# Moving the halves of a record from ScalarE's scaled block one-hots to VectorE's scaled place one-hots in a graph kernel

## The chip, the cores and the metric

The kernel runs on one core of a Trainium2 chip. The metric is the device time of one launch in microseconds. The engines are called PE (TensorE), DVE (VectorE), ACT (ScalarE), POOL (GpSimd) and SP (SyncE), as the profile calls them; PEld is PE's loading of the stationary operand.

## What is computed

20,000 nodes carry 256 numbers each, and 340,000 edges are sorted by their destination. A relational layer is applied twice, then an attention layer:

```python
def _rgcn_layer(x, W, self_w, b, src, dst, edge_type, num_nodes):
    xW = jnp.einsum('ni,rio->rno', x, W)
    msg = xW[edge_type, src]
    agg = jax.ops.segment_sum(msg, dst, num_segments=num_nodes)
    return agg + x @ self_w + b
...
x = layernorm(x + rgcn(relu(rgcn(x))))          # 8 edge types
# attention: here the segments are the sources (row = src), the gathered rows those of dst
e = leaky_relu(hl[row] + hr[col]); att = softmax of e within each row; out[row] += att * h[col]
x = layernorm(x + out)
```

The relational layers sum over edges that end in a node, the attention layer over edges that start in one. So the edges, given in order of destination, must also be brought into order of source.

## The kernel before

**Rounds one and two** are the two relational layers (`by_chunks`). The edges lie in 2657 columns ("tiles") of 128, and 16 tiles make a chunk. For each tile POOL gathers 128 rows by an indirect DMA (L536), 20 tiles ahead in 24 buffers. PE multiplies the gathered rows by one-hots of destination and type that DVE makes (L556), summing into PSUM (L653). ACT and DVE copy the finished sums (L578, L576). PE then multiplies them by the weights: L588 turns the chunk's own rows, L591 (ACT) copies them, L596 and L600 are the products. In round one `use` goes on with L723 to L731, in round two with L762 to L796.

**The order by source** (`ordered`) runs beside the rounds, a piece at a time: after most tiles `pace` lets the generator `side` advance by one `yield`, four times in five tiles in round one from some tile on, five times in eight in round two. The stage that the change touches is `write`, called `the write stage` below. It works on lots of three tiles, and each lot takes three such steps. The sources fall into 157 blocks of 128 nodes; a record is a pair of node and source place in one integer, cut into two halves `hi` and `lo` that fp16 holds exactly. For one tile, with edges on the partitions:

- `blocks_of` (L849, DVE) makes `b`, the one-hot of an edge's block: 128x157 fp16 for each of the three tiles, in one instruction of 471 columns. `b` has 4 buffers.
- `rank` (L1005, L1006, PE) counts, by two products into `pr`, how many edges of the same block come before each edge.
- `place_of` (DVE) takes that count out of `pr` at the edge's block (L1026, three times), takes 128 off where it passes 127 (L1029, L1030), and makes `a`, the one-hot of the place, 128x384 fp16 for a whole lot (L1032). `a` has 3 buffers.
- `parts` (ACT) makes `two`: `b` times `hi` (L1016) and `b` times `lo` (L1017), for each tile; 7 buffers.
- `bring` (PE) adds the transposed `a` times `two` into `pl`, 314 columns for each tile (L1044): every half of a record lands at its place and block.
- `finish` joins the halves and turns and stores a group's records when all its tiles are in.

`pi`, the row of column numbers that `a` and `b` compare with, lies in PSUM as f32. All instructions of an engine run in the order in which the program gives them; the order is written out by hand (`manual_schedule`). In `write` the order for lot m is: `parts(m + 1, 0)` and where a group begins `begin`; a step of `finish`; end of step; `blocks_of(m + 2)`, `parts(m + 1, 1)`, a step of `finish`; end of step; `bring(m)`, `parts(m + 1, 2)`, `rank(m + 1)`, `place_of(m + 1)`; end of step. So PE brings a lot one lot's time after DVE was asked for its places.

**Attention** follows the rounds: for each of 157 blocks POOL gathers 17 tiles of rows (L1252), and PE, DVE and ACT work through them (L1262 to L1399). The change doesn't touch it.

Of the kernel before, what the change touches and what calls it, by code (L numbers as in the profile page):

```python
# [38 lines left out]
FP16 = mybir.dt.float16  # L39
AF = mybir.ActivationFunctionType  # L40
ALU = mybir.AluOpType
# [6 lines left out]
P = 128  # L48
# [13 lines left out]
LOT = 3  # L62
# [4 lines left out]
def gnn_kernel(  # L67
# [17 lines left out]
    nc = tc.nc  # L85
# [5 lines left out]
    NB = (N + P - 1) // P  # L91
# [24 lines left out]
    G = -(-COLS // GT)  # L116
# [686 lines left out]
    class ordered:  # L803
# [171 lines left out]
        def write(self, sp, ps, pi):  # L975
            k = self.k
            lots = self.lots
            held = sp.tile([P, NB], F32, name="held", bufs=1)
            nc.vector.memset(held, 0.0)
            group, made, ranked, later = {}, {}, {}, []  # L980
            pl = [None]

            def begin(g):


                x = ps.tile([P, 512], F32, name="pr")[:, :3 * NB].rearrange("p (a b) -> p a b", a=3)
                nc.tensor.matmul(x[:, 0, :], self.below16, self.count_all[:, g, :], start=True, stop=False)
                of = self.ident16[:, g:g + 1].to_broadcast([P, P])
                nc.tensor.matmul(x[:, 0, :], of, self.place16, start=False, stop=True)
                nc.tensor.matmul(x[:, 1, :], of, self.place16, start=True, stop=True)  # L990
                nc.tensor.matmul(x[:, 2, :], of, self.cross16, start=True, stop=True)
                start = sp.tile([P, NB], FP16, name="start")
                nc.scalar.copy(start, x[:, 0, :])
                cross = sp.tile([P, NB], F32, name="cross")
                nc.scalar.copy(cross, x[:, 2, :])
                mine = sp.tile([P, NB], F32, name="mine")
                nc.vector.tensor_scalar(mine, x[:, 1, :], self.row, None, op0=ALU.is_le)
                group[g] = start, cross, mine

            def rank(m):  # L1000
                g, i, n, _ = lots[m]
                pr = ps.tile([P, 512], F32, name="pr")[:, :LOT * NB].rearrange("p (x b) -> p x b", x=LOT)
                self.pending = True
                for x in range(n):
                    nc.tensor.matmul(pr[:, x, :], self.below16, made[m][:, x, :], start=True, stop=False)  # L1005
                    nc.tensor.matmul(pr[:, x, :], self.ident16[:, i + x:i + x + 1].to_broadcast([P, P]), group[g][0],  # L1006
                                     start=False, stop=True)
                ranked[m] = pr

            def parts(m, x):  # L1010
                g, i, n, _ = lots[m]
                if x >= n:
                    return
                c = g + G * (i + x)
                two = sp.tile([P, 2, NB], FP16, name="two", bufs=2 * LOT + 1)
                nc.scalar.activation(two[:, 0, :], made[m][:, x, :], AF.Copy, scale=k["hi"][:, c:c + 1])  # L1016
                nc.scalar.activation(two[:, 1, :], made[m][:, x, :], AF.Copy, scale=k["lo"][:, c:c + 1])  # L1017
                ranked[m, x] = two

            def place_of(m):  # L1020
                g, i, n, _ = lots[m]
                pr = ranked.pop(m)
                r = sp.tile([P, LOT], F32, name="r")
                for x in range(n):
                    dump = sp.tile([P, NB], FP16, name="dump")
                    nc.vector.tensor_tensor_reduce(out=dump, in0=pr[:, x, :], in1=made[m][:, x, :], scale=1.0,  # L1026
                                                   scalar=0.0, op0=ALU.mult, op1=ALU.max, accum_out=r[:, x:x + 1])
                over = sp.tile([P, LOT], F32, name="rover")
                nc.vector.tensor_scalar(over[:, :n], r[:, :n], float(P), -float(P), op0=ALU.is_ge, op1=ALU.mult)  # L1029
                nc.vector.tensor_add(r[:, :n], r[:, :n], over[:, :n])  # L1030
                a = sp.tile([P, LOT, P], FP16, name="a16", bufs=3)
                nc.vector.tensor_tensor(a[:, :n], pi[:, :P].unsqueeze(1).to_broadcast([P, n, P]),  # L1032
                                        r[:, :n].unsqueeze(2).to_broadcast([P, n, P]), op=ALU.is_equal)
                ranked[m] = a

            def bring(m):
                g, i, n, of = lots[m]
                if i == 0:
                    while later:
                        one()  # L1040
                    pl[0] = ps.tile([P, 512], F32, name="pl")[:, :2 * NB].rearrange("p (a b) -> p a b", a=2)
                a = ranked.pop(m)
                for x in range(n):
                    nc.tensor.matmul(pl[0].rearrange("p a b -> p (a b)"), a[:, x, :],  # L1044
                                     ranked.pop((m, x)).rearrange("p a b -> p (a b)"),
                                     start=(i + x == 0), stop=(i + x == of - 1))
                made.pop(m)
                if i + n == of:
                    later.extend(finish(g, pl[0]))
# [47 lines left out]
            def one():  # L1097
                if later:
                    later.pop(0)()

            begin(0)
            for m in (0, 1):
                if m < len(lots):
                    made[m] = self.blocks_of(sp, pi, lots[m])
            rank(0)
            place_of(0)
            for x in range(LOT):
                parts(0, x)
            for m in range(len(lots)):
                more = m + 1 < len(lots)  # L1110
                self.pending = False
                if more:
                    parts(m + 1, 0)

                    if lots[m + 1][1] == 0:
                        begin(lots[m + 1][0])
                        self.pending = True
                one()
                yield
                self.pending = False  # L1120
                if m + 2 < len(lots):
                    made[m + 2] = self.blocks_of(sp, pi, lots[m + 2])
                if more:
                    parts(m + 1, 1)
                one()
                yield
                bring(m)
                if more:
                    for x in range(2, LOT):
                        parts(m + 1, x)  # L1130

                    rank(m + 1)
                    place_of(m + 1)
                yield
# [62 lines left out]
    def attention():  # L1197
        with tc.tile_pool(name="ac", bufs=1) as cp, tc.tile_pool(name="ag", bufs=4) as gp, \
# [204 lines left out]
            def step(i):  # L1403
# [29 lines left out]
                if b and not a:  # L1433

                    weights(b)
                    for t in range(0, b["n"] + 1, 6):
                        weigh_few(b, list(range(t, min(t + 6, b["n"] + 1))))
                        sums(b, range(t, min(t + 6, b["n"] + 1)))
                    if c:
                        sums(c, [17])  # L1440
                        finish(c)
                        measure(c)
                        write(c)
                    finish(b)
                    measure(b)
                    write(b)
                    return
# [19 lines left out]
                for n in range(1, 10):  # L1467
                    if b:
                        sums(b, [n])
                        weigh(b, [n + 4] + ([14, 15] if n == 9 else []))  # L1470
                    if a:
                        greatest(a, (n + 2) // 4, (n + 2) % 4)
                        if n == 5:
                            turned_hots(a)
                    if n in (2, 4, 6, 8):
                        load_ob(i + 2, n // 2)
                    if c and n == 1:
                        measure(c)
                    if c and n == 4:
                        write(c)  # L1480
# [303 lines left out]
    with tc.tile_pool(name="rows", bufs=1) as keep:  # L1784
        k = {}
# [35 lines left out]
```

## Time and profile before

| | |
|---|---|
| time, median of 3 runs | 10404.4 us (10398.89 to 10406.65) |
| profiled execution: its own time | 14109.72 us |
| its span, first to last instruction | 14107.9 us |
| first and last gather of round one and two (L536) | 67.2 and 8681.5 us |
| write stage, first and last product L1044 | 2016 and 8375 us |
| first gather of attention (L1252) | 8724.7 us |
| busy in the span: PE, PEld, DVE, ACT, POOL | 10231.6, 7774.8, 7641.1, 6176.7, 7657.7 us |
| granted TensorE clock, mean | 0.849 of full speed |

The profiled execution took 1.356 times as long as the runs that were timed without the profiler. A duration below is one of the profiled execution. Busy time of PE is modelled, since matmuls overlap; where a rate is wanted, starts are subtracted from starts.

### The profile page before, as it was taken

What the parts mean: (1) busy time and instruction counts of PE and PEld (TensorE: products, weight loads), DVE (VectorE), ACT (ScalarE), POOL (GpSimd) and SP (SyncE); (2) the same over time, 40 slices, a digit from 0 to 9 for tenths busy, and PEclk for the clock granted to TensorE, in tenths of its full rate; (3) what the DMA queues carried; (4) which work ended last, traced back from release to release, by engine and by line L of the source; (5) the groups of instructions that cost most, each with busy time, mean ns of one, the idle gap of its engine ahead of it and who ended that gap; (6) DMA issues with size and microseconds to landing.
All of it is one profiled execution on the core that took longest, in us unless ns stands there. A gap on an engine that the chain in (4) does not pass through costs nothing. (4 is left out here: it accounts for less than half of the span.)

```text
span 14107.9 us, 225925 instructions
## 1 busy us (share of the span) xinstructions
PE 10231.6 (73%) x78029; PEld 7774.8 (55%) x78029; DVE 7641.1 (54%) x21279; ACT 6176.7 (44%) x19534; POOL 7657.7 (54%) x8057
## 2 busy tenths in 40 slices
PE   6888888888887888888888885555555555555555
PEld 5777777777776666766676664333333333333333
DVE  4455555555555555555555542555555555555555
ACT  2211124444443333333333331656656666656656
POOL 5665666665565555555555555444444444444443
PEclk8998999999998999999999997777777777777777
DMA  6654544454444445554555454333333333333332
GB/s 187 181 144 139 143 139 142 142 142 141 141 141 137 142 142 144 143 145 140 143 145 143 143 146 134 92 97 95 101 96 96 100 97 99 97 97 97 98 98 81
DMA packets 859356, 1788.95 MB, mean 127 GB/s; under 512 B 200612, under 2 KB 521746, under 8 KB 858050
## 3 DMA queue, kind: packets, MB, share of 16 engines
q0 software_dynamic: 464336, 1396.47, 36.0%
q1 hardware_dynamic: 387490, 371.40, 8.4%
q8 instruction: 613, 10.04, 0.3%
q10 hardware_dynamic: 6368, 6.54, 0.1%
q14 instruction: 549, 4.50, 0.1%
HBM read 1638.71 MB, written 135.15 MB: 126 GB/s over the span
## 5 line engine op out<-in xcount | busy, mean ns | idle before, releaser
L1252 POOL DMA_INDIRECT g<-table3s,to x2657 | 2565.0, 965 | 2795.4 <-PE po L1362 1547.0
L536 POOL DMA_INDIRECT g<-h2s,idx x2657 | 2517.8, 948 | 1889.1 <-PE a L653 1084.8
L653 PE MATMUL a<-s,g 128*128 128x184 bf16 (+14 forms) x37024 | 3180.2, 231 | 137.7 <-issue 123.6
L1348 ACT ACTIVATE g<-g 128x64 f32<-128x64 f32 x9984 | 2620.4, 336 | 1047.1 <-issue 1024.3
L600 PE MATMUL pm<-wt,to 128*128 128x256 f32 x10624 | 3020.0, 408 | 8.2 <-issue 7.9
L536 POOL DMA_INDIRECT g<-xs,idx x2305 | 2195.3, 952 | 1445.9 <-PE a L653 786.5
L1306 DVE CUSTOM_DVE_ANT_0 dump<-pr,pen 128x768 bf16<-128x768 f32 x1876 | 1654.4, 908 | 2109.4 <-remote 1659.7
L653 PEld LDWEIGHTS <-g 128*128 128x128 bf16 x35352 | 2487.4, 101 | 452.2 <-issue 198.8
L1303 PE MATMUL pr<-hpt,pick 128*128 128x512 bf16 (+2 forms) x3752 | 1007.5, 355 | 2219.3 <-issue 1124.2
L1362 PE MATMUL po<-g,s 128*128 128x260 f32 x5314 | 2014.4, 477 | 99.5 <-DVE g L1354 83.5
L600 PEld LDWEIGHTS pm<-wt,to 128*128 128x128 f32 x10624 | 1902.5, 199 | 231.8 <-issue 53.9
L1303 PEld LDWEIGHTS <-pick 128*128 128x128 bf16 x3752 | 388.1, 103 | 2812.9 <-issue 2697.2
L578 ACT COPY to<-a 128x512 f32<-128x512 f32 x996 | 564.2, 586 | 2979.5 <-PE a L653 2466.3
L1026 DVE CUSTOM_DVE_ANT_0 dump<-pr,b 128x157 f16<-128x157 f32 x2657 | 713.6, 320 | 1958.2 <-PE pr L1006 777.5
L1016 ACT ACTIVATE two<-b,hi 128x157 f16<-128x157 f16 x2657 | 1121.1, 422 | 410.5 <-DVE b L849 214.5
L1362 PEld LDWEIGHTS po<-g,s 128*128 128x128 f32 x5314 | 1003.5, 229 | 522.8 <-issue 179.1
L849 DVE TENSOR_TENSOR b<-pi,kb 128x471 f16<-128x471 f32 (+1 forms) x1798 | 1113.0, 634 | 274.0 <-PE pr L891 103.1
L1017 ACT ACTIVATE two<-b,lo 128x157 f16<-128x157 f16 x2657 | 1099.2, 414 | 0.0
L556 DVE TENSOR_TENSOR s<-pi,code 128x1600 bf16<-128x1600 f32 (+1 forms) x622 | 1022.2, 1644 | 0.0
L596 PE MATMUL pm<-wt,ot 128*128 128x256 f32 x1328 | 506.7, 518 | 513.8 <-issue 307.1
L1292 ACT CAST hpt<-pr 12x768 bf16<-12x768 f32 (+1 forms) x469 | 350.2, 747 | 929.0 <-PE pr L1290 852.4
L1044 PE MATMUL pl<-two,a 128*128 128x314 f16 x2657 | 537.5, 313 | 173.7 <-DVE a L1032 73.3
(279 smaller groups left out, 10148.5 us busy)
## 6 DMA issues: line engine op xcount, KB each, us to landing
ob<-ownd SPq DMA_DIRECT2D x625, 128.0 KB
g<-h2s,idx POOLq DMA_INDIRECT x2657
g<-table3s,to POOLq DMA_INDIRECT x2657
y<-in_x SPq DMA_DIRECT2D x321, 128.0 KB
g<-xs,idx POOLq DMA_INDIRECT x2305
h2s<-h SPq DMA_DIRECT2D x166, 192.0 KB
own<-h2s SPq DMA_DIRECT2D x166, 192.0 KB
xs<-xs SPq DMA_DIRECT2D x156, 192.0 KB
```

The costliest lines, as they stand in the source:

```text
L536: nc.gpsimd.indirect_dma_start(out=g, out_offset=None, in_=of, in_offset=bass.IndirectOffsetOnAxis(ap=idx[:, u:u + 1], axis=0))
L556: nc.vector.tensor_tensor(s, pi[:, :w].unsqueeze(1).to_broadcast([P, e - f, w]), code[:, c:c + e - f].unsqueeze(2).to_broadcast([P, e - f, ...
L600: nc.tensor.matmul(p, sums[:, i % 2, i // 2, :], wt[:, i % 2, i // 2, :], start=False, stop=(i == 2 * R - 1))
L653: nc.tensor.matmul(a[h, q][:, b:e, :].rearrange("p n r -> p (n r)"), g[:, v * D + h * P:v * D + (h + 1) * P], s, start=((h, q) not in begu ...
L849: nc.vector.tensor_tensor(b[:, :n], pi[:, :NB].unsqueeze(1).to_broadcast([P, n, NB]), self.k["kb"][:, c:c + G * (n - 1) + 1:G].unsqueeze(2 ...
L1016: nc.scalar.activation(two[:, 0, :], made[m][:, x, :], AF.Copy, scale=k["hi"][:, c:c + 1])
L1017: nc.scalar.activation(two[:, 1, :], made[m][:, x, :], AF.Copy, scale=k["lo"][:, c:c + 1])
L1252: nc.gpsimd.indirect_dma_start(out=g[:, t, :], out_offset=None, in_=table3s, in_offset=bass.IndirectOffsetOnAxis(ap=to3[:, b, t:t + 1], ax ...
L1303: nc.tensor.matmul(pr[:, t:t + n, :], pick[:, h, :], k["hpt"][:, q + t:q + t + n, :], start=True, stop=True)
L1306: nc.vector.tensor_tensor_reduce(out=dump[:, :m, :].rearrange("p t e -> p (t e)"), in0=pr[:, :m, :].rearrange("p t e -> p (t e)"), in1=k[" ...
L1348: nc.scalar.activation(gh[:, h, :], gh[:, h, :], AF.Copy, scale=k["g"][:, t, D + h:D + h + 1])
L1362: nc.tensor.matmul(k["po"], k["s"][:, t, :] if t < n else ident, k["g"][:, t, :SR], start=(t == 0), stop=(t == n))
```

## The change

`parts`, the buffers `two` and ACT's two instructions per tile go. `place_of` no longer makes a lot's `a` by one comparison of 384 columns but by six instructions of 128 columns, two for each tile: one compares the column numbers with the place `r` and multiplies by `hi`, the other by `lo`. Both `r` and the half are pointers to one value per partition. `a` becomes twice as large, still in 3 buffers. `bring` makes two products of 157 columns for each tile instead of one of 314, each with a stationary operand of its own and with `b` itself as the moving one, into the two halves of `pl`.

```diff
-            def parts(m, x):
-                g, i, n, _ = lots[m]
-                if x >= n:
-                    return
-                c = g + G * (i + x)
-                two = sp.tile([P, 2, NB], FP16, name="two", bufs=2 * LOT + 1)
-                nc.scalar.activation(two[:, 0, :], made[m][:, x, :], AF.Copy, scale=k["hi"][:, c:c + 1])
-                nc.scalar.activation(two[:, 1, :], made[m][:, x, :], AF.Copy, scale=k["lo"][:, c:c + 1])
-                ranked[m, x] = two
...
-                a = sp.tile([P, LOT, P], FP16, name="a16", bufs=3)
-                nc.vector.tensor_tensor(a[:, :n], pi[:, :P].unsqueeze(1).to_broadcast([P, n, P]),
-                                        r[:, :n].unsqueeze(2).to_broadcast([P, n, P]), op=ALU.is_equal)
+                a = sp.tile([P, LOT, 2, P], FP16, name="a16", bufs=3)
+                for x in range(n):
+                    c = g + G * (i + x)
+                    for v, of in enumerate((k["hi"], k["lo"])):
+                        nc.vector.tensor_scalar(a[:, x, v], pi[:, :P], r[:, x:x + 1], of[:, c:c + 1],
+                                                op0=ALU.is_equal, op1=ALU.mult)
...
                 for x in range(n):
-                    nc.tensor.matmul(pl[0].rearrange("p a b -> p (a b)"), a[:, x, :],
-                                     ranked.pop((m, x)).rearrange("p a b -> p (a b)"),
-                                     start=(i + x == 0), stop=(i + x == of - 1))
+                    for v in range(2):
+                        nc.tensor.matmul(pl[0][:, v, :], a[:, x, v], made[m][:, x, :],
+                                         start=(i + x == 0 and v == 0), stop=(i + x == of - 1), skip_group_check=True)
...
-            for x in range(LOT):
-                parts(0, x)
...
-                if more:
-                    parts(m + 1, 0)
...
-                if more:
-                    parts(m + 1, 1)
...
-                    for x in range(2, LOT):
-                        parts(m + 1, x)
```

More of the change, by code (lines that the diff above doesn't have):

```diff
@@ L1111, in write @@
                 self.pending = False
-                if more:
-                    parts(m + 1, 0)
-                    if lots[m + 1][1] == 0:
-                        begin(lots[m + 1][0])
-                        self.pending = True
+                if more and lots[m + 1][1] == 0:
+                    begin(lots[m + 1][0])
+                    self.pending = True
                 one()
```

## Prediction, made before the result

> **What bounds the kernel now.** I read the page's first part, then the stretches of the write stage (the busy time by stretch), then the waits of PE and DVE in it, then the instructions in order of time. From the page:
>
> ```profile
> PE 10231.6 (73%) x78029; PEld 7774.8 (55%) x78029; DVE 7641.1 (54%) x21279; ACT 6176.7 (44%) x19534; POOL 7657.7 (54%) x8057
> L1026 DVE CUSTOM_DVE_ANT_0 dump<-pr,b 128x157 f16<-128x157 f32 x2657 | 713.6, 320 | 1958.2 <-PE pr L1006 777.5
> L1016 ACT ACTIVATE two<-b,hi 128x157 f16<-128x157 f16 x2657 | 1121.1, 422 | 410.5 <-DVE b L849 214.5
> L1017 ACT ACTIVATE two<-b,lo 128x157 f16<-128x157 f16 x2657 | 1099.2, 414 | 0.0
> L1044 PE MATMUL pl<-two,a 128*128 128x314 f16 x2657 | 537.5, 313 | 173.7 <-DVE a L1032 73.3
> ```
>
> The shares mix stages, so the first stretch below is round one's part of the write stage, the second round two's (columns: length, then PE, PEld, DVE, ACT, POOL busy, clock, DMA share, GB/s):
>
> ```profile
> 2050.00:4150.00 2100.00, 1774.40 (x16247) 1484.69 (x16247) 1226.06 (x4104) 925.74 (x2655) 1260.67 (x1328) 0.93 0.50 142
> 4250.00:8350.00 4100.00, 3407.73 (x29683) 2827.57 (x29682) 2119.93 (x7371) 1544.29 (x4348) 2337.60 (x2467) 0.91 0.50 143
> ```
>
> PE is busy for 84% and 83%; DVE for 58% and 52%, ACT for 44% and 38%. ACT, whose work goes, is the least loaded. PE's own waits in the first stretch (total us, times, longest):
>
> ```profile
> PE pl L1044 <- DVE a L1032: 54.4, 34, 4.2
> PE pm L596 <- ACT ot L591: 38.7, 14, 4.7
> PE pl L1044 <- DVE r L1030: 19.1, 11, 2.9
> PE pl L1044 <- DVE rover L1029: 8.8, 5, 3.4
> PE pl L1044 <- ACT two L1017: 6.2, 4, 1.9
> PE pm L596 <- ACT two L1017: 2.2, 2, 1.3
> ```
>
> PE waits for DVE's places, 82.3 us in 50 of the 354 lots; for `two` it waits 8.4 us. So PE sets the pace and the late hand is DVE's, at the very instructions that grow.
>
> **The second limit is POOL.** In the profile's order of time its gathers, where nothing holds them, start 1.25 us apart (0.95 us each and 0.30 us of issue). The kernel has 2657 x 3 = 7971 gathers: 9964 us of POOL's pace. The timed runs take 10404.4 us, the profiled one 14109.7, so most of what the profiler adds must lie where the gathers are slow in the profile: 2485 in 5000 us of attention, 2.01 us each, while the rounds take 1.58 and 1.66. Attention can't be below 2657 x 1.25 = 3321 us plus an edge, the 66 us after its last gather. So the rounds have about 10404 - 67 - 3321 - 66 = 6950 us, or 1.31 us a tile, against POOL's 1.25. I estimate that unprofiled PE and POOL are within 5% of each other in the rounds. A PE loss then reaches the end nearly whole, a PE gain only as far as POOL follows: 5314 x 0.06 = 320 us at most.
>
> **What the Trainium skill says.** *VectorE: DVE Perf Modes*, "Why PSUM operands drop a tier": an f32 PSUM operand keeps DVE at one element a cycle. `pi` is one, so 128 columns cost 133 ns at 0.96 GHz plus a fixed part. The trace agrees: L1032 needs 475 ns start to start for 384 columns, 400 + 75. *TensorE: Matmul & The Clock Gate*, "Wait — 56ns, not 53.3ns?": warm matmuls follow each other at N/2.4 GHz + 2.5 ns, 68 ns for 157 columns; in the trace L1005 and L1006 start 0.07 us apart although each loads other weights. *SBUF — State Buffer*, "Who interferes with whom": a DVE instruction with at most one SBUF input outside the two-port modes doesn't contend with GpSimd; the new ones read their stream from PSUM, so I charge POOL's descriptors nothing. No view of before shows this form beside a gather.
>
> **DVE, added.** These are the rows of one lot (start, duration):
>
> ```profile
> 2014.74 0.32 DVE L1026 CUSTOM_DVE_ANT_0 dump<-pr,b 128x157 f16<-128x157 f32 x1
> 2014.99 0.08 DVE L1026 DVE_READ_ACCUMULATOR2_ANT r<- 128x1 f32 x1
> 2015.10 0.17 DVE L1029 TENSOR_SCALAR rover<-r 128x3 f32<-128x3 f32 x1
> 2015.31 0.16 DVE L1030 TENSOR_TENSOR r<-r,rover 128x3 f32<-128x3 f32 x1
> 2015.50 0.56 DVE L1032 TENSOR_TENSOR a<-pi,r 128x384 f16<-128x384 f32 x1
> 2015.98 0.64 DVE L849 TENSOR_TENSOR b<-pi,kb 128x471 f16<-128x471 f32 x1
> ```
>
> Out goes 0.475 us per lot (2015.98 less 2015.50, rounded). In come six of 128 columns. The form with two pointers isn't in the trace; the nearest row is L997, a pointer comparison of 157 PSUM columns, which takes 0.26 us at its quickest and 0.38 as a median. Lower bound: 133 ns and no gap, 0.80 us a lot, +0.33. Upper bound: 0.38 less 30 ns for the fewer columns and 75 of overlap, about 0.28, 1.68 a lot, +1.2. I take L1032's slope and gap, 0.21: 1.26 us a lot, **+0.785**. Over all it is 5314 x 0.21 = 1116, less some 422 us for L1032's 899 instructions at their own lengths: +694 us of DVE. A lot of round one has 2100/354 = 5.9 us in the profile and, at 1.31 instead of 1.58 us a tile, 4.9 unprofiled; DVE's 3.46 us become 4.25, 87% of it. In round two a lot has 7.9 us, unprofiled 6.3, and DVE's 4.1 become 4.9, 78%.
>
> **What is queued behind it.** `place_of` ends a lot's DVE work; behind it stand `blocks_of`, the gather one-hots L556 (1.5 to 1.8 us each, for PE's L653), the copy L576, and `left`, `y` and the norms. DVE waits at L1026 for PE's ranks in 282 of 354 lots of the first stretch, 681 us in all, 2.4 us each. That slack hides most of the 0.785. It does not where DVE comes late: the 72 lots without a wait.
>
> - Round one: the 50 waits of PE for DVE each come later by up to 0.785 for the longer one-hots and again by 0.785 for a lot carried late: 50 x 1.57 = 79 us. A further 46 lots (0.785/4.8 of 282, with the slack spread evenly to 4.8 us) come late by 0.4: 18 us. Together +97.
> - Round two: PE waits for L1032, L1030 and L1029 are only some 12 us there, but L790 waits 156.9 us, 76 times, for `pr` to be read by L1026. A third of these delayed by 0.785 is 20 us, as much again for new ones: +40.
>
> **PE.** Three products start 0.41 us before what follows them (4001.28 to 4001.69): 0.137 each. Six of 0.068 are 0.41. The 2657 more weight loads lie under the products as for L1005 and L1006: nothing, and if that cover is gone, six loads of 0.05 or so, 0.15 us a lot more than today, 135 us. I keep this for the range.
>
> **ACT.** 1121 + 1099 = 2220 us go. It is not the bound; what counts is what it held up. In the first stretch L1016 sits 177 us waiting for `b`, with copies behind it. Worth to PE: the 8.4 us for `two`, the share of L596 with `two` directly ahead of `ot` (some 23 us of the 38.7), and a little of DVE's 49 us for L723's `h`: **-35 us**. Round two adds little: there ACT was idle before most late `ot`. No DMA is moved or added, and SP's queue is not passed. The new wait, PE on each `a`, is on the same engine as today; `b` is now freed by PE's L1044 rather than ACT's L1016, but its fourth buffer leaves a lot's time, so nothing. After the change no ACT wait for `b` remains.
>
> **The sum.** 97 + 40 - 35 = +102 us on the profiled 14109.7 us, about 14,210. The timed median is 26% below that execution and much of the difference is attention, so I carry microseconds, not per cent, and let POOL absorb a quarter: +76, **10,480 us**.
>
> **Rivals.**
>
> - *ACT's release wins* (0.22, faster). The mechanism: `two` stands in front of `to`, `ot` and `h` on ACT, and PE, short of PSUM and of `ot`, restarts sooner. For it: 42 waits of `left` for `h`, 12 of PE behind `two`. Against: ACT at 44%, with 469 us waiting for L653. It decides if DVE's new form is at the lower bound (+0.33 hides in 2.4 us) and half of L596's 111 us and of round two's are ACT's doing: 35 + 60 less 20, about -75: 10,330.
> - *POOL hides it* (0.13, no change). If gathers set the pace even in the rounds, PE's +102 is taken up by 20 tiles of advance; 10,410. Against: POOL waits 478 us for L653 in the first stretch.
> - *DVE becomes the bound of round one* (0.2 of the slower chance). It decides from about 0.28 us an instruction: 3.46 + 1.2 = 4.66 of 4.9 us, every compare late, 383 lots x 0.5 + 516 x 0.15 = +270: 10,675. That weight loads show is the same size and adds to it.
>
> **How the numbers follow.** Slower 0.65 (0.45 by the sum, 0.2 with DVE as bound), same 0.13, faster 0.22. About 0.2%, 21 us, is what a measurement of this kernel can tell from no change. The range runs from 10,360, within the faster case, to 10,680: it leaves out a tenth at each side. The slower cases alone would be 10,425 to 10,680.
>
> **What would show it.** L1016 and L1017 gone, ACT's share near 28%; a `TENSOR_SCALAR` group of 5314 with about 0.23 us each and 0.21 start to start; DVE some 700 us busier, its waits at L1026 shorter by a third; PE's wait L1044 <- L1032's successor above 130 us in round one; PE busy unchanged. It is wrong if PE's waits for DVE don't grow, if L596's waits halve, or if the new form takes 0.15 or 0.3 us.

## The result and the profile after

The changed kernel takes 11,015.42 us (median of 4 runs, 11,012.75 to 11,023.66) against 10,405.52 for the kernel before: **5.9% slower**, ratio 1.0587 with a 95% interval of 1.0574 to 1.0599, or +610 us. The forecast was slower, but 10,480 us and 10,680 at most.

The profiled execution after took 11,023.66 us, close to its timed runs, while the profiled execution of before that the prediction rests on took 14,109.72, 1.356 times its timed runs. So the kernel before was profiled once more, in a launch that took 10,412.79 us, and the comparison below is made with that one. That execution was profiled too, so the profiler is not the reason for the longer one, as the prediction took it to be. Launches of these programs run at two levels, the kernel before at 10,405 or at 13,939 us, so a time is compared only with that of the kernel before in the same launch. From the pages, first of the changed kernel (one execution; the columns are busy us, share and instructions, then the groups of instructions with mean ns and idle time before):

```profile
PE 9518.6 (86%) x80686; PEld 7456.9 (68%) x80686; DVE 8772.3 (80%) x25694; ACT 4242.9 (38%) x14220; POOL 7689.8 (70%) x8057
L1016 DVE CUSTOM_DVE_ANT_0 dump<-pr,b 128x157 f16<-128x157 f32 x2657 | 710.9, 319 | 571.8 <-PE pr L1006 571.0
L1026 DVE TENSOR_SCALAR a<-pi,r,hi 128x128 f16<-128x128 f32 x2657 | 1073.2, 404 | 32.8
L1026 DVE TENSOR_SCALAR a<-pi,r,lo 128x128 f16<-128x128 f32 x2657 | 1065.2, 401 | 0.0
```

and of the kernel before, profiled again:

```profile
PE 9217.8 (89%) x78029; PEld 7226.0 (69%) x78029; DVE 7537.6 (72%) x21279; ACT 5928.4 (57%) x19534; POOL 7698.7 (74%) x8057
L1026 DVE CUSTOM_DVE_ANT_0 dump<-pr,b 128x157 f16<-128x157 f32 x2657 | 711.3, 319 | 873.9 <-PE pr L1006 872.9
```

ACT lost its two groups, 2225 us by their durations and 1686 of its busy time, since the two overlap. DVE gained 1235 us, and its wait for the ranks fell from 874 to 572 us: part of the new work went into that slack. The number to look at is the mean of 401 to 404 ns for a comparison of 128 columns; the prediction expected about 230.

All the loss lies in the rounds. From the gathers of the traces: round one's last gather starts at 3460 us before and 3673 after (+213); round two lasts from 3500 to 6911 before and from 3722 to 7530 after (3412 against 3808 us, +396); from there to the end it is 3500 us before and 3492 after. The stretches of the write stage, first round one's part and then round two's (length, PE, PEld, DVE, ACT, POOL busy, clock, DMA share, GB/s), after:

```profile
1750.00:3500.00 1750.00, 1647.77 (x16161) 1376.56 (x16159) 1583.31 (x5470) 231.42 (x521) 1179.29 (x1240) 0.98 0.55 159
3750.00:7150.00 3400.00, 3069.93 (x29855) 2672.97 (x29853) 2659.99 (x9431) 536.68 (x1257) 2236.96 (x2369) 0.97 0.57 164
```

and before, profiled again:

```profile
1750.00:3450.00 1700.00, 1659.84 (x16562) 1430.15 (x16560) 1229.56 (x4192) 933.41 (x2716) 1287.01 (x1356) 0.99 0.63 179
3550.00:6550.00 3000.00, 2900.10 (x28200) 2505.32 (x28201) 1977.48 (x6987) 1442.28 (x4118) 2228.11 (x2353) 1.00 0.66 185
```

POOL's count is the number of tiles. Before, a tile takes 1700/1356 = 1.25 us in round one, which is the 1.25 us from one gather to the next where nothing holds POOL, and 1.27 in round two; after, 1.41 and 1.44. DVE went from 72% to 90% busy in round one, from 66% to 78% in round two. The granted clock fell in round two from 1.00 to 0.97, but that explains little: L600's products follow each other every 0.236 us in the mean in both stretches, L653's every 60 and 62 ns, some 25 us over its 15,000 products.

**Round one: the weight loads wait.** PE's busy share hardly shows the loss, 98% before and 94% after, because a wait of the weight load can lie within the time that is booked for the products. Here, after the change, six products are booked as 1.84 us of work without a gap, while the loads under them wait for one one-hot after the other (start, duration, in brackets the idle time before):

```profile
3275.33 1.84 PE L1039 MATMUL pl<-b,a 128*128 128x157 f16 x6
3275.65 0.10 PEld L1039 LDWEIGHTS <-a 128*128 128x128 f16 x1 [0.22 <-DVE a L1026]
```

Where `a` is there, the six are booked as 0.58. The waits of PEld in round one's stretch show it, after and then before:

```profile
PEld L1039 <- DVE a L1026: 172.2, 665, 1.2
```

```profile
PEld L1044 <- DVE a L1032: 32.1, 74, 0.9
```

665 short waits of 0.26 us: in these lots PE reaches the products while DVE is still at the six one-hots and takes each as it comes, although by the program's order DVE had a whole lot's time for them. 172 - 32 = 140 us is most of what the stretch lost (1.411 - 1.254 = 0.157 us x 1240 tiles = 195).

**Round two: another chain.** PE's waits there, after and then before (400 us less in length):

```profile
PE pr L782 <- ACT x L775: 228.4, 96, 2.9
PE pr L790 <- DVE r L1016: 56.7, 44, 1.3
```

```profile
PE pr L782 <- ACT x L775: 75.3, 92, 1.3
PE pr L790 <- DVE r L1026: 2.1, 3, 0.9
```

In order of time, after (start, duration, in brackets the idle time before):

```profile
4876.39 0.41 DVE L1026 TENSOR_SCALAR a<-pi,r,hi 128x128 f16<-128x128 f32 x1
4876.71 0.40 DVE L1026 TENSOR_SCALAR a<-pi,r,lo 128x128 f16<-128x128 f32 x1
...
4877.99 0.40 DVE L1026 TENSOR_SCALAR a<-pi,r,lo 128x128 f16<-128x128 f32 x1
4878.31 0.15 DVE L771 RECIPROCAL rs<-rs 128x1 f32<-128x1 f32 x1
4878.49 0.16 DVE L772 SCALAR_TENSOR_TENSOR rs<-mv,rs 128x1 f32<-128x1 f32 x1
...
4878.69 0.60 ACT L775 ACTIVATE x<-y,rs 128x256 f32<-128x256 f32 x1 [3.66 <-DVE rs L772]
...
4879.34 0.44 PE L782 MATMUL pr<-ident,x 128*128 128x128 f32 x2 [2.93 <-ACT x L775]
```

The starts lie 0.32 us apart. The reciprocal of the norm, one column, stands behind all six, ACT stands 3.66 us for it, and PE 2.93 us for ACT. The two waits of PE, at L782 and L790, make some 208 us more than before, of about 380 that the stretch lost (1.435 - 1.275 = 0.16 us x 2369 tiles); the rest isn't assigned to a wait.

### The profile page after: what moved, and what is told of

Read it like the earlier page. It is cut to its first block, busy times and chain, and to the rows that moved or that the text cites. A ratio compares the mean times of both kernels' runs of the same rounds, so it can differ in the third digit from the quotient of the medians.

```text
span 11021.9 us, 229722 instructions
## 1 busy us (share of the span) xinstructions
PE 9518.6 (86%) x80686; PEld 7456.9 (68%) x80686; DVE 8772.3 (80%) x25694; ACT 4242.9 (38%) x14220; POOL 7689.8 (70%) x8057
## 4 chain that ended last, share of the span: by engine, by line
PE 40%; DVE 29%; POOL 10%; issue 10%; ACT 5%; DMA 5%; SPq 0%; DVEq 0%; ACTq 0%; POOLq 0%
PE pm L600 18%; PE a L653 10%; POOL g L1238 10%; DVE a L1026 8%; DVE dump L1016 4%; DVE b L849 3%; DVE dump L1292 3%; ACT g L1334 3%; DMA g<-table3s,to 2%; DVE s L556 2%; PE pl L1039 2%; PE pm L596 2%; PE pr L790 1%; DMA xs<-xs 1%; PE po L1348 1%
## 5 line engine op out<-in xcount | busy, mean ns | idle before, releaser
L653 PE MATMUL a<-s,g 128*128 128x184 bf16 (+14 forms) x37024 | 3060.0, 228 | 24.2 <-DMA own<-in_x 10.8
L600 PE MATMUL pm<-wt,to 128*128 128x256 f32 x10624 | 2888.6, 395 | 0.7 <-DVE to L576 0.7
L653 PEld LDWEIGHTS <-g 128*128 128x128 bf16 x35352 | 2405.9, 99 | 288.1 <-issue 29.2
L1334 ACT ACTIVATE g<-g 128x64 f32<-128x64 f32 x9984 | 2435.4, 334 | 5.1
L600 PEld LDWEIGHTS pm<-wt,to 128*128 128x128 f32 x10624 | 1819.3, 191 | 181.6 <-issue 3.8
L1348 PE MATMUL po<-g,s 128*128 128x260 f32 x5314 | 1728.7, 417 | 81.9 <-DVE g L1340 51.3
L1348 PEld LDWEIGHTS po<-g,s 128*128 128x128 f32 x5314 | 851.4, 196 | 421.7 <-ACT g L1334 90.2
L1026 DVE TENSOR_SCALAR a<-pi,r,hi 128x128 f16<-128x128 f32 x2657 | 1073.2, 404 | 32.8
L1026 DVE TENSOR_SCALAR a<-pi,r,lo 128x128 f16<-128x128 f32 x2657 | 1065.2, 401 | 0.0
L1039 PE MATMUL pl<-b,a 128*128 128x157 f16 x5314 | 707.3, 242 | 99.8 <-DVE a L1026 34.5
L1039 PEld LDWEIGHTS <-a 128*128 128x128 f16 x5314 | 456.4, 101 | 337.2 <-DVE a L1026 255.8
L1276 PE MATMUL pr<-identb,g 128*12 128x128 bf16 x2657 | 267.2, 221 | 309.3 <-DMA g<-table3s,to 264.4
```

Of the source, the lines that this page charges most:

```text
L600: nc.tensor.matmul(p, sums[:, i % 2, i // 2, :], wt[:, i % 2, i // 2, :], start=False, stop=(i == 2 * R - 1))
L653: nc.tensor.matmul(a[h, q][:, b:e, :].rearrange("p n r -> p (n r)"), g[:, v * D + h * P:v * D + (h + 1) * P], s, start=((h, q) not in begu ...
L1026: nc.vector.tensor_scalar(a[:, x, v], pi[:, :P], r[:, x:x + 1], of[:, c:c + 1], op0=ALU.is_equal, op1=ALU.mult)
L1039: nc.tensor.matmul(pl[0][:, v, :], a[:, x, v], made[m][:, x, :], start=(i + x == 0 and v == 0), stop=(i + x == of - 1), skip_group_check=True)
L1334: nc.scalar.activation(gh[:, h, :], gh[:, h, :], AF.Copy, scale=k["g"][:, t, D + h:D + h + 1])
L1348: nc.tensor.matmul(k["po"], k["s"][:, t, :] if t < n else ident, k["g"][:, t, :SR], start=(t == 0), stop=(t == n))
```

## The experiments

**The kernel before again (no edit).**

> The kernel before once more, for a profiled execution that lies near its timed 10,405 us, as that of the changed kernel does near its own. If attention takes what it takes in the changed kernel (3492 us from the rounds' last gather to the end), the rounds take 10,405 - 3,492 - 67 = 6,846 us, 1.29 us a tile, against 7,463 us or 1.40 after. All theories: ACT near 58% of the span, DVE near 0.85 to 0.9 us a tile in round one's write stage. The theory that DVE's time is the cause wants DVE's waits at the ranks near 300 us per 1,000 us there; the rival that PE's products are the cause wants PE with 5% or more to spare.

Measured: 10,412.79 us; the rounds end at 6911 us, 6845 us after the first gather, as expected; DVE 0.91 us busy a tile in round one. PE has not 5% to spare there but 2%, and DVE's wait at the ranks is 302 us in 1700, 178 per 1000 and so below the 300 that theory A wanted. Neither theory's sign came: DVE had less slack than thought, and so had PE.

**PE's part alone.**

```diff
-                    nc.tensor.matmul(pl[0].rearrange("p a b -> p (a b)"), a[:, x, :],
-                                     ranked.pop((m, x)).rearrange("p a b -> p (a b)"),
...
+                    two = ranked.pop((m, x))
+                    for v in range(2):
+                        nc.tensor.matmul(pl[0][:, v, :], a[:, x, :], two[:, v, :],
...
...
```

> PE's part of the change alone: six products of 157 columns a lot with six weight loads, while ACT still scales the block one-hots and DVE makes the places by one comparison. Theory A (DVE's instructions cost the time): 10,380 to 10,440 us, no change. Rival B (the smaller products and their weight loads cost the time): 10,700 to 11,015 us.

Measured: 10,411.6 us, ratio 1.0004 (0.9995 to 1.0013). The smaller products and their weight loads cost nothing; rival B falls.

**DVE's part alone.**

```diff
+                for y in range(6):
+                    x, v = y // 2 % n, y % 2
+                    c = g + G * (i + x)
+                    spare = sp.tile([P, P], FP16, name="spare", bufs=6)
+                    nc.vector.tensor_scalar(spare, pi[:, :P], r[:, x:x + 1], (k["hi"], k["lo"])[v][:, c:c + 1],
+                                            op0=ALU.is_equal, op1=ALU.mult)
                 a = sp.tile([P, LOT, P], FP16, name="a16", bufs=3)
```

> DVE's part alone: ahead of the comparison of 384 columns DVE makes the six scaled one-hots of 128 columns as well, into a spare buffer that nothing reads; ACT and PE as before. DVE gets 6 x 0.319 = 1.91 us a lot more than before, where the change adds 1.91 - 0.475 = 1.44. Theory A: slower than the changed kernel, 11,100 to 11,350 us. Rival B: 10,405 to 10,500 us.

Measured: 11,392.92 us, ratio 1.0946 (1.0928 to 1.0964), above the changed kernel and slightly above the range. Work that nobody reads, on DVE alone, costs what the change costs and more. PE's largest wait in round one's stretch (2100 us; total, times, longest) is the one for the comparison behind the spare ones:

```profile
PE pl L1050 <- DVE a L1038: 295.7, 177, 3.0
```

**What the instruction costs by its parts.** Spare instructions behind each lot's comparison, two of each form: L1040 with two pointers from PSUM, L1042 with one, L1044 with none, L1046 with two from f32 in SBUF, L1048 with two from fp16 in SBUF, L1052 for both halves of a tile.

```diff
+                nc.vector.tensor_scalar(d[0], pi[:, :P], r[:, 0:1], hi, op0=ALU.is_equal, op1=ALU.mult)
...
+                nc.vector.tensor_scalar(d[2], pi[:, :P], r[:, 0:1], None, op0=ALU.is_equal)
...
+                nc.vector.tensor_single_scalar(d[4], pi[:, :P], 5.0, op=ALU.is_equal)
...
+                nc.vector.tensor_scalar(d[6], iota, r[:, 0:1], hi, op0=ALU.is_equal, op1=ALU.mult)
...
+                nc.vector.tensor_scalar(d[8], self.iota16, r[:, 0:1], hi, op0=ALU.is_equal, op1=ALU.mult)
...
+                    nc.vector.scalar_tensor_tensor(both, pi[:, :P].unsqueeze(1).to_broadcast([P, 2, P]), r[:, 0:1],
+                                                   k["hi"][:, :2].unsqueeze(2).to_broadcast([P, 2, P]),
+                                                   op0=ALU.is_equal, op1=ALU.mult)
```

> What the new instruction costs by its parts: behind each lot's comparison DVE makes spare one-hots that nothing reads, two of each form, the start of one to the start of the next read from the trace. Two pointers, column numbers f32 in PSUM (the form of the change): 0.32 us. If the pointers are dear: one pointer 0.26, none 0.20, and with the column numbers in SBUF and two pointers still about 0.3. If PSUM is dear: 0.32 with one pointer or none too, and 0.2 or less from SBUF. One instruction for both halves of a tile (256 columns, comparison with a pointer, then times a second tensor): 0.42 if its fixed part is that of the other two-tensor instructions, 0.55 if it carries the pointers' price. The time itself is far above 11,015 us, for DVE gets some 3 us a lot.

Measured: 12,236.69 us. From the groups of instructions of that run (busy us, mean ns):

```profile
L1052 DVE SCALAR_TENSOR_TENSOR spares<-pi,r,hi 128x256 f16<-128x256 f32 x1798 | 779.3, 473 | 0.0
L1040 DVE TENSOR_SCALAR spare<-pi,r,hi 128x128 f16<-128x128 f32 x899 | 360.3, 401 | 0.0
L1046 DVE TENSOR_SCALAR spare<-iota,r,hi 128x128 f16<-128x128 f32 x899 | 307.9, 342 | 0.0
L1042 DVE TENSOR_SCALAR spare<-pi,r 128x128 f16<-128x128 f32 x899 | 306.3, 341 | 0.0
L1048 DVE TENSOR_SCALAR spare<-iota,r,hi 128x128 f16<-128x128 f16 x899 | 300.6, 334 | 0.0
L1044 DVE TENSOR_SCALAR spare<-pi 128x128 f16<-128x128 f32 x899 | 250.2, 278 | 0.0
```

401, 341 and 278 ns with two, one and no pointer; start to start, by the median of the trace, 0.319, 0.258 and 0.198 us. **A pointer costs 0.06 us**: between L1042 and L1044 it is the only difference. Between L1040 and L1042 the second operation, the multiplication, goes as well as the second pointer; that step is 0.06 too, and no run separates the two. Without a pointer the form costs about what the prediction took for it. From SBUF the two-pointer form takes 0.253 (f32) and 0.223 (fp16), so PSUM has a part too. One instruction for two halves takes 0.395, less than the 0.638 of a pair like L1026's.

**Two launches with the kernel before at 13,939 us.** Their edits are those of the runs below: ACT's scaling kept, one instruction per tile, column numbers in SBUF, two more steps before the norm's turn, three spare one-hots.

> The changed kernel, with ACT still scaling the block one-hots into a buffer that nothing reads: what ACT's release was worth. Theory A (DVE's time alone counts): 11,000 to 11,040 us, as the changed kernel. Rival C (the change gained by freeing ACT and lost more on DVE): 11,080 us or above.

> The changed kernel with one instruction per tile instead of two: the column numbers are compared with the place and multiplied by a second tensor that holds hi and lo, 256 columns at 0.395 us start to start (from the run of forms). DVE gets 3 x 0.395 - 0.475 = 0.71 us a lot more than before, where the change adds 1.44 and the run with six spare one-hots 1.91. The changed kernel's 610 us and that run's 986 lie on a line of 790 us for each microsecond a lot, which begins at 0.67. Theory A: 10,405 to 10,520 us, 10,440 by the line. Rival B' (PE's many small products cost once ACT's scaling is gone): 10,700 us or above.

> The changed kernel with the column numbers as fp16 in SBUF instead of f32 in PSUM: 0.223 us start to start for each of the six, 0.86 us a lot more than before. Theory A by the same line: 10,555 us, between 10,480 and 10,620. If this form holds up POOL's gathers, as some of its durations of 0.5 us hint: L536's gathers longer than 0.95 us and 10,650 us or above.

> The changed kernel with two more steps in round two between the norm and its turn on PE (L775 to L782). In the changed kernel the reciprocal L771 stands behind a lot's six one-hots, and PE waits 231 us for L775 in round two's write stage. Theory A2 (round two loses by this chain): that wait all but goes, 10,780 to 10,860 us, round one unchanged. Rival D (DVE's total work bounds round two too): 10,990 to 11,030 us, and the wait turns up at L1039 or L653.

> One instruction per tile again, for a launch in which the kernel before takes its 10,405 us: DVE gets 0.71 us a lot more than before. Theory A, by the line that begins at 0.67: 10,440 us, between 10,405 and 10,520. Rival B' (the small products cost once ACT's scaling is gone): 10,700 us or above.

> The changed kernel with two more steps before the norm's turn, again in such a launch. Theory A2: 10,780 to 10,860 us, PE's 231 us of waiting at L782 for L775 nearly gone, round one unchanged. Rival D (DVE's work bounds round two too): 10,990 to 11,030 us.

> The changed kernel with ACT's scaling kept, again in such a launch. Theory A: 11,000 to 11,040 us. Rival C (freeing ACT gained something back): 11,080 us or above.

> The kernel before with three spare scaled one-hots a lot ahead of the comparison, 3 x 0.319 = 0.96 us a lot more than before. By the line that begins at 0.67 with 790 us for each microsecond a lot: 10,630 us. If the cost has no threshold, 986 x 0.96 / 1.91 = 493 us: 10,900. Rival B: 10,405 to 10,440.

Measured, as ratios to the kernel before in the same launch: ACT kept 0.9984 (0.9976 to 0.9992) and 0.9993 (0.9984 to 1.0002); one per tile 0.9968 (0.9955 to 0.9981) and 0.9984 (0.9976 to 0.9991); SBUF columns 0.9965 (0.9956 to 0.9974); later turn 1.0048 (1.0032 to 1.0064) and 1.0064 (1.0047 to 1.0081); three spare 0.9965 (0.9949 to 0.9981). None of the expected differences is there. In executions of this length PE, PEld and ACT have gaps that the profile puts down to `issue`, so to no wait that it shows, and DVE has some that it puts down to `remote`. The same line of attention in the page of the prediction's profile, which ran at this level, and then of the kernel before profiled again:

```profile
L1348 ACT ACTIVATE g<-g 128x64 f32<-128x64 f32 x9984 | 2620.4, 336 | 1047.1 <-issue 1024.3
```

```profile
L1348 ACT ACTIVATE g<-g 128x64 f32<-128x64 f32 x9984 | 2435.4, 334 | 5.1
```

In the first run with ACT kept the rounds took 8464 us here. DVE's added time may find room in the gaps; what makes them was not settled, and that it is they that hide it was not tried. These two launches ran on two chips, and the launches of all the other runs of this section on three more, so that the chip may be what makes the difference is not excluded. The runs below repeat these edits beside a kernel before of 10,405 us.

**One instruction per tile.** `both` is one buffer in which `hi` and `lo` now lie side by side.

```diff
...
-                    for v, of in enumerate((k["hi"], k["lo"])):
-                        nc.vector.tensor_scalar(a[:, x, v], pi[:, :P], r[:, x:x + 1], of[:, c:c + 1],
-                                                op0=ALU.is_equal, op1=ALU.mult)
+                    nc.vector.scalar_tensor_tensor(
+                        a[:, x], pi[:, :P].unsqueeze(1).to_broadcast([P, 2, P]), r[:, x:x + 1],
+                        k["both"][:, :, c:c + 1].bitcast(F32).to_broadcast([P, 2, P]), op0=ALU.is_equal, op1=ALU.mult)
```

> One instruction per tile, for a launch in which the kernel before takes 10,405 us: DVE gets 0.71 us a lot more than before, the small products and the freed ACT stay. Theory A, by the line that begins at 0.67: 10,440 us, between 10,405 and 10,520. Rival B' (the small products cost once ACT's scaling is gone): 10,700 us or above. Where the kernel before takes 13,939 us instead: as before within 0.5%.

Measured: 10,614.12 us, ratio 1.020 (1.018 to 1.022). Two thirds of the loss go with half of DVE's added time, but +208 us is above theory A's range: the line with a threshold at 0.67 is wrong, the cost begins earlier. It is below rival B''s range as well; whether the small products have a part in the 208 us is for the kernels further down that leave them out.

**A later turn in round two.**

```diff
             nc.scalar.activation(x1, y, AF.Identity, bias=rs[:, 1:2], scale=rs[:, 0:1])
             yield
             yield
+            yield
+            yield
             yield True
```

> The changed kernel with two more steps before the norm's turn on PE. Theory A2: 10,780 to 10,860 us where the kernel before takes 10,405, PE's waiting at L782 for L775 nearly gone, round one unchanged. Rival D (DVE's work bounds round two too): 10,990 to 11,030 us. Where the kernel before takes 13,939 us instead: 0 to 1% above it.

Measured: 10,969.69 us, ratio 1.054 (1.0519 to 1.056): 46 us less than the changed kernel, of the 228 that PE waited there. PE's wait for `x` did go: in this stretch no row names L775 any more, and at the turn (L784 in this kernel's lines) PE waits 17 us, for L1018. But the waits of PE and of PEld in round two's stretch show what came instead:

```profile
PE pm L596 <- ACT ot L591: 106.8, 75, 3.6
```

```profile
PEld L1041 <- DVE a L1028: 164.3, 680, 1.6
```

L596 had no wait in this stretch after the change, and PEld waited 40.5 us for `a`. The wait at L596 is the same reciprocal by another way:

```profile
4872.76 0.60 ACT L775 ACTIVATE x<-y,rs 128x256 f32<-128x256 f32 x1 [3.67 <-DVE rs L772]
...
4873.73 0.37 ACT L591 COPY ot<-pm 128x256 f32<-128x256 f32 x1
...
4874.16 1.13 PE L596 MATMUL pm<-wt,ot 128*128 128x256 f32 x4 [0.65 <-ACT ot L591]
```

ACT stands for L772, and `ot` stands behind `x` in ACT's order; so it is at each of the 75 waits. The edit moved PE's use of `x`, not the reciprocal behind the six one-hots. The time lies between the ranges of theory A2 and rival D, and the run doesn't decide between them: one part of the wait came back through the same chain, another as PEld's wait for the one-hots themselves. The reciprocal ahead of the six one-hots on DVE, which would separate the two, was not tried.

**ACT's scaling kept**, into buffers that nothing reads, in the places it had.

```diff
...
+                nc.scalar.activation(two[:, 0, :], made[m][:, x, :], AF.Copy, scale=k["hi"][:, c:c + 1])
+                nc.scalar.activation(two[:, 1, :], made[m][:, x, :], AF.Copy, scale=k["lo"][:, c:c + 1])
...
```

> The changed kernel with ACT's scaling kept, unread. Theory A (ACT's release is worth nothing): 11,000 to 11,040 us where the kernel before takes 10,405. Rival C (it gained something back): 11,080 us or above.

Measured: 11,019.71 us, ratio 1.0591 (1.0573 to 1.0609), the changed kernel's time. Freeing ACT of some 2200 us is worth nothing that can be measured.

**Three spare one-hots.** The edit of the six, with three.

> The kernel before with three spare scaled one-hots a lot, 0.96 us of DVE more a lot, ACT and PE as before. The three amounts measured so far (0.71 us: +208; 1.44: +610; 1.91: +986) bend upwards; between them 0.96 gives +330, so 10,700 to 10,770 us if DVE's time alone decides. If the freed ACT or the small products had a part in the changed kernel's and the one-per-tile form's times, it lies outside: a threshold at 0.67 would give 10,630, no bend 10,900.

Measured: 10,764.97 us, ratio 1.0342 (1.0325 to 1.036), +356 us, within the range. ACT and PE do the same work as before in this kernel, so DVE's time alone gives the point.

**The later turn in the kernel before.** The same two steps.

> The kernel before with the two more steps before the norm's turn on PE. In it PE waits 75 us for L775 in 3,000 us of round two. If that wait is worth its time, 10,300 to 10,360 us; if PE then waits for ot at L596 or POOL's pace of 1.25 us a tile takes it, 10,390 to 10,420.

Measured: 10,415.46 us, ratio 1.0006 (0.9998 to 1.0015). No change: PE now waits 28 us at L596 and 35 us at the turn and at the product behind it, instead of 75 for the norm. None of the kernels at this level beats the kernel before.

**Column numbers as fp16 in SBUF.**

```diff
...
-                        nc.vector.tensor_scalar(a[:, x, v], pi[:, :P], r[:, x:x + 1], of[:, c:c + 1],
+                        nc.vector.tensor_scalar(a[:, x, v], self.iota16, r[:, x:x + 1], of[:, c:c + 1],
```

> The changed kernel with the column numbers as fp16 in SBUF: six of 0.223 us, 0.86 us of DVE a lot more than before. By the bent line through the four amounts measured (0.71: +208; 0.96: +356; 1.44: +610; 1.91: +986) +290, so 10,670 to 10,730 us. If the form, in which DVE reads its stream from SBUF, also holds up POOL's gathers: 10,750 us or above, with L536's mean well over 0.95 us.

Measured: 10,711.01 us, ratio 1.029 (1.0273 to 1.0307), +299 us, as expected from DVE's time. The page of that run:

```profile
L536 POOL DMA_INDIRECT g<-h2s,idx x2657 | 2516.2, 947 | 1103.1 <-PE a L653 532.8
L536 POOL DMA_INDIRECT g<-xs,idx x2305 | 2191.9, 951 | 838.5 <-PE a L653 367.2
```

The gathers take 947 and 951 ns as before (947 and 952 in the kernel before, profiled again): this form does not hold POOL up.

**The five amounts together.** DVE's added time a lot, and what it cost the kernel:

| kernel | DVE added, us a lot | time, us | added, us |
|---|---|---|---|
| one instruction per tile | 0.71 | 10,614 | +208 |
| fp16 columns in SBUF | 0.86 | 10,711 | +299 |
| three spare | 0.96 | 10,765 | +356 |
| the change | 1.44 | 11,015 | +610 |
| six spare | 1.91 | 11,393 | +986 |

They rise together, whatever ACT and PE do beside them. As an estimate, a curve through zero and the two kernels that only add DVE work, three and six spare, gives 240, 310 and 640 us for the other three, against 208, 299 and 610 measured: so freeing ACT and the smaller products together took away some 30 us at the most. With 5314/6 = 886 lots' worth of instructions, 1.44 us a lot is some 1273 us of DVE, of which 610 reach the end.

## Why the prediction was wrong

- **The size of the new instruction** is the first step that failed: "I take L1032's slope and gap, 0.21". It measured 0.319, so a lot got 1.44 us instead of 0.785. The slope and gap were right for a form without pointers (0.198); the two pointers, with the multiplication, add 0.12. The bound from above, 0.28, came from L997, which has one pointer: the one-pointer form measured 0.258. So the reading of L997's median of 0.38 us was sound, but for one pointer. A bound from a row with one of two operands is no bound. The reading of *VectorE: DVE Perf Modes* ("Why PSUM operands drop a tier"), one element a cycle from PSUM, agrees with 0.198 us, which is its 0.133 for 128 columns and a fixed 0.065; what no row showed was the price of the pointers and the second operation.
- **From DVE's time to PE's waits** is the second. The step put +137 us of waits on +0.785 us a lot (97 + 40). The amounts measured give about +250 there (between +208 at 0.71 and +299 at 0.86). "That slack hides most" was read from DVE's waits of 2.4 us in 282 of 354 lots, in an execution of 14,110 us. These 681 us are the sum of all rows of L1026: 188 us of it names the ranks, L1006, and 137 are `remote` and `issue`. I scaled the length of a lot to the timed runs but not the slack. In the execution of 10,413 us DVE waits at L1026 for PE's ranks for 302 us in 199 of 361 lots of the same stage, 1.5 us each, and PE waits for L1032 only 14.9 us in 35 of them: neither the slack nor the 50 late lots of the longer execution are those of the timed runs. The wait that was to show it, above 130 us at PE, came as PEld's 172 us; PE's own row has 23.6. With the size corrected alone, each term scaled to 1.44 us, the sum gives 144 + 61 + 73 - 35 = +243 us, not +610; the rest is this step's.
- **Round two**, charged +40, lost 396, most of the whole. The text named "`left`, `y` and the norms" as queued behind the one-hots and then priced only L790. L771 behind them is what PE waited for at L782, and, when the turn was moved, by way of ACT at L591; in the execution of 14,110 us PE already waited 57.3 us at L782 for `x` in that stretch. A queue that is named has to be costed at each of its consumers.
- **ACT's release**, -35 us: zero. That ACT was not the bound was right. The waits that the term was made of belonged to the longer execution: in that of 10,413 us PE waits for `two` once, 1.1 us, and in round one's stretch not at all for `ot`.
- **PE at nothing** was right: PE's part alone is within 0.1%, and in that run the products of 157 columns follow each other every 0.068 us (median), as *TensorE: Matmul & The Clock Gate* ("Wait — 56ns, not 53.3ns?") has it. **POOL's descriptors at nothing** was right as well: round two's gathers take 945 ns in the mean after and 947 before, which agrees with *SBUF — State Buffer* ("Who interferes with whom") for a form with its stream from PSUM.
- **Attention and the rounds apart**: the estimate of 6950 us for the rounds, 1.31 us a tile, stands against 6845 and 1.29, with 1.25, POOL's own, in round one. That PE and POOL are both near their limits there was right; it fits that so little of DVE's time was hidden, though no run shows that it is the reason.
- Of the rivals, "DVE becomes the bound of round one" had the mechanism; its +270 us was too small for the same reason as the sum and left round two nearly out, and its threshold of 0.28 us an instruction is not seen: the cost rises from the smallest amount tried.

## What to carry to other kernels

Price an instruction by a row with all of its operands: a comparison of 128 columns cost 0.198 us bare and 0.319 with two per-partition pointers and a multiplication, and six of these for one large instruction cost 5.9%. Before using waits of a profile as cover, compare the profiled execution's own time with the timed runs; where it is longer, don't take its slack for theirs (here 681 us in 2100 against 302 in 1700). Moving work from an engine at 44% to one at 58% is decided by who waits for the second engine's results, in every stage that shares it; removing one such wait by itself gave back a fifth of it, and where the late result has a second way to the waiting engine, that way has to be found first.

## What was not expected of the hardware

- A per-partition pointer costs DVE 0.06 us (0.198 and 0.258 us start to start at 128 columns from PSUM); a second one with a second operation costs 0.06 us more (0.319).
- A wait of PE's weight load hides in PE's busy time: in round one PE is 94% busy, and its weight loads wait 172 us of 1750 for `a`. The waits of PEld show it.
- The same program was profiled in 10,413 and in 14,110 us, the longer with 1024 us of ACT's gaps at `issue` before L1348 alone; what makes them stays open.
